# Attention's output projection for two tiles as seven block products instead of eight (Strassen's scheme), with the weights and sums of them streamed in pieces

## The chip, the cores and the metric

The kernel runs on one core of one Trainium2 chip. The metric is device microseconds (us) of one execution, and what is compared is the median of several executions. The engines of the core are named as in the profile: PE is TensorE (matmul), PEld its weight load, DVE is VectorE, ACT is ScalarE, POOL is GpSimd, SP is SyncE. SP and POOL issue the DMA transfers of the part that matters here (SPq is SP's issue queue).

## The reference, cut to what is computed

The model is three layers over `x` of 64 sequences x 32 tokens x 512 features (2048 rows), all in float32. The change lies in the third layer's attention (32 query heads, 8 key heads, 128 per head, a paged cache of 512 keys per sequence), in the last line of this:

```
q = rope(rmsnorm(x @ Wq.T));  k = rope(rmsnorm(x @ Wk.T));  v = x @ Wv.T
probs = softmax(where(valid, q k_all * SCALE, -1e30))
o = einsum('bhqk,bkhd->bqhd', probs, v_all).reshape(bsz, seqlen, HQ * D)
return einsum('bse,de->bsd', o, Wo)
```

`o` is 2048 x 4096 and `Wo` is 512 x 4096: the output projection is a product of 2048 x 4096 by 4096 x 512. A second feed-forward part follows it (the class `Tail` in the kernel).

## The kernel before, in words

**Order of the layers.** `layer0`, `layer1`, then `attention`, whose last act is `tail.run()`, the feed-forward part behind attention. TensorE's instructions have a fixed order: `on_pe` (line 82) ties each one to the one emitted before it. The instructions of the other engines and of the queues are placed by the framework's scheduler when the program is built, by priority in the order of emission and by its estimate of what is ready, so their order can differ a little from the order of the code.

**Steps.** Attention goes over the heads in two halves (`HALVES`, 16 query heads and 4 key heads each) and in each half over 16 tiles of 128 rows (4 sequences): 32 steps (line 858). A step has 16 turns, one for each sequence (4) and key head of the half (4). Turn `i` transposes the softmaxed scores (`turned`, line 805), emits the scores of turn `i + 2` (`scores`, line 779: two matmuls, a DVE reduction, ACT's exponential, a DVE reciprocal and a DVE scaling) and multiplies probabilities by values (`values`, line 820). The tile `sc` in PSUM has one buffer, so a turn's scores can be written once DVE has reduced those before.

**Slots.** Between these pieces each turn has two slots, 32 in a step (line 933): lists of small functions that are emitted there. They hold the projections of the next step (`Projection.product`, six products of two parts each: v, k and four groups of q), the transposes of its queries and keys (`turned`, line 742), loads, and the output projection of the step before (`Output.product`, line 757).

**The output projection.** For one tile and one half it is 16 matmuls (one for each head) of 128 x 128 stationary (`oT`, attention's output, transposed) by 128 x 512 moving (`wo`): eight parts of two heads, accumulated in one PSUM tile `py`, at slots 18, 19, 21, 23, 25, 27, 29, 31 of the following step; the parts of step 30 at the odd slots up to 15 of step 31, and those of step 31 behind the loop (lines 994 to 998). Behind the eighth part DVE copies the result (first half of the heads) or adds what the first half had stored (`y_before`), and SP stores it. `wo` (16 x 512 for each of 128 partitions, one half of the heads) stays in SBUF: it is loaded in four transfers of 1024 KB at the start and in four more between the halves (`output_weights`, line 852). In the profile every float32 matmul of the code is two MATMUL instructions, so a part is four instructions.

**Keys and values.** The keys of a sequence come as 16 transfers of 64 KB by SP, one for each page (`load_keys`, line 649, `kts` has two buffers), emitted at the second turn of the sequence two before; the values come as four indirect transfers by POOL (`load_values`, line 659).

## Time and profile before

| what | value |
|---|---|
| three runs | 3680.55, 3685.11, 3684.99 us; median 3684.99 us |
| the profiled execution's own time | 3681.84 us |
| its span, first to last instruction | 3679.8 us |
| busy: PE, DVE, ACT, POOL | 3631.7, 1805.6, 1316.3, 1254.1 us |
| granted clock of TensorE, mean | 0.999 |
| attention, 1062 to 3509.3 us of the span: PE busy | 2437.35 of 2447.30 us |
| the output projection's matmuls (`py<-wo,oT`, x1024): PE busy | 480.3 us |
| mean share of the 16 DMA engines in attention | 0.44, at 130 GB/s |

How to read it: matmuls are pipelined and the page models their ends, so the records of two neighbours overlap, and the mean duration of one (593 ns for 512 columns) is longer than the distance from its start to the next. Where the prediction needs the cost of a matmul, it takes that distance, from views in order of time. The clock of 0.999 says that PE ran unthrottled throughout. Idle time of an engine that is not the bottleneck costs nothing, so the 480.3 us of the output projection count in full and most of the other engines' times don't.

### The profile page before, as it was taken

The numbers are of one execution on the slowest core, as the hardware profiler recorded it, in microseconds if no ns is written. First come the engines' busy times: TensorE is split into PE (matmuls) and PEld (weight loads), VectorE is DVE, ScalarE is ACT, GpSimd is POOL, SyncE is SP. The second block draws the span as 40 slices with busy tenths as digits, with TensorE's granted clock in tenths as the row PEclk, the third lists the DMA queues.
The fourth block names the chain that finished last, engine by engine and source line by source line (L and its number), as shares of the span: only waits on it lengthen the run. The fifth ranks groups of instructions, "written<-read, shape, count | busy, mean of one in ns | idle before, by whom it ended". The sixth has DMA issues, their size and how long they took to land.

```text
span 3679.8 us, 62184 instructions
## 1 busy us (share of the span) xinstructions
PE 3631.7 (99%) x18752; PEld 2523.7 (69%) x18752; DVE 1805.6 (49%) x4815; ACT 1316.3 (36%) x3014; POOL 1254.1 (34%) x1265
## 2 busy tenths in 40 slices
PE   8999999999999999999999999999999999999999
PEld 3444788888867776777777776777777777777755
DVE  5452222222236655565556655566555655566423
ACT  1111111111125444444444444444444444444411
POOL 0112100000035444544445444444444444454222
PEclk9999999999999999999999999999999999999999
DMA  5014211111144444344443355544444344444521
GB/s 209 23 35 162 92 44 60 44 47 34 37 141 134 124 122 122 117 116 116 123 122 118 115 184 179 165 132 119 123 123 125 117 123 122 129 120 123 160 68 61
DMA packets 410062, 407.70 MB, mean 111 GB/s; under 512 B 49954, under 2 KB 322338, under 8 KB 409730
## 3 DMA queue, kind: packets, MB, share of 16 engines
q1 hardware_dynamic: 363010, 251.65, 22.5%
q0 software_dynamic: 44416, 147.88, 13.2%
q10 hardware_dynamic: 2304, 4.20, 0.3%
q8 instruction: 153, 2.51, 0.3%
q14 instruction: 179, 1.47, 0.1%
HBM read 382.57 MB, written 20.97 MB: 110 GB/s over the span
## 4 chain that ended last, share of the span: by engine, by line
PE 89%; SPq 1%; DMA 0%; DVE 0%; issue 0%; ACT 0%; POOL 0%; ACTq 0%; POOLq 0%; DVEq 0%
PE po L640 14%; PE sc L791 13%; PE pq L640 12%; PE py L640 12%; PE gate_up L311 10%; PE prT_ps L635 6%; PE pz L311 5%; PE po L1100 3%; PE pv L640 3%; PE pk L640 3%; PE po L311 2%; PE qkT_ps L635 2%; PE pd L247 1%; PE ph L122 1%; SPq L93 0%
## 5 line engine op out<-in xcount | busy, mean ns | idle before, releaser
L662 POOL DMA_INDIRECT vt<-in_v_rows,v_rows x512 | 500.7, 978 | 816.7 <-PE po L640 708.8
L640 PEld LDWEIGHTS po<-prT,vt 128*128 128x128 f32 x4096 | 530.1, 192 | 183.7 <-issue 178.0
L796 DVE CUSTOM_DVE_ANT_0 pr<-sc,mask 128x544 f32<-128x544 f32 x512 | 369.2, 721 | 458.7 <-PE sc L791 457.5
L798 ACT ACTIVATE pr<-pr,low 128x544 f32<-128x544 f32 x512 | 383.4, 749 | 540.7 <-DVE low L796 536.4
L791 PE MATMUL sc<-kt,qT 128*128 128x288 f32 (+1 forms) x2048 | 555.1, 394 | 5.2 <-ACT qT L748 2.4
L640 PE MATMUL po<-prT,vt 128*128 128x128 f32 x4096 | 540.8, 275 | 1.6 <-ACT prT L809 1.6
L791 PEld LDWEIGHTS sc<-kt,qT 128*128 128x128 f32 x2048 | 369.2, 191 | 180.8 <-issue 106.9
L640 PE MATMUL py<-wo,oT 128*128 128x512 f32 x1024 | 480.3, 593 | 0.7 <-ACT oT L839 0.7
L640 PE MATMUL pq<-wq,xT 128*128 128x512 f32 x1024 | 480.9, 593 | 0.0
L809 ACT COPY prT<-prT_ps 128x512 f32<-128x512 f32 x512 | 298.5, 583 | 272.6 <-PE prT_ps L635 269.4
L803 DVE TENSOR_SCALAR pr<-pr,low 128x512 f32<-128x512 f32 x512 | 364.5, 712 | 16.7
L635 PE MATMUL prT_ps<-ident,pr 128*128 128x128 f32 x2048 | 310.9, 275 | 1.3 <-DVE pr L803 1.3
L640 PEld LDWEIGHTS py<-wo,oT 128*128 128x128 f32 x1024 | 192.6, 191 | 137.5 <-issue 125.6
L640 PEld LDWEIGHTS pq<-wq,xT 128*128 128x128 f32 x1024 | 182.8, 191 | 129.9 <-issue 125.1
L800 DVE RECIPROCAL low<-low 128x1 f32<-128x1 f32 x512 | 83.5, 163 | 360.6 <-ACT pr L798 359.6
L635 PEld LDWEIGHTS prT_ps<-ident,pr 128*128 128x128 f32 x2048 | 237.7, 141 | 9.1 <-issue 1.5
L126 POOL TENSOR_TENSOR rs<-rs,minus_half 128x4 f32<-128x4 f32 x160 | 166.2, 1039 | 167.4 <-DVE rs L678 166.1
L694 POOL TENSOR_TENSOR rot<-rot,swapped 128x512 f32<-128x512 f32 x160 | 202.7, 1267 | 1.0
L801 ACT ACTIVATE own_pr<-pr,low 128x32 f32<-128x32 f32 x512 | 164.2, 321 | 106.3 <-DVE low L800 104.2
L695 POOL TENSOR_TENSOR rot<-rot,rs 128x512 f32<-128x512 f32 x160 | 177.1, 1107 | 8.0
L395 DVE TENSOR_TENSOR sg<-sg,gate_up 128x256 f32<-128x256 f32 (+1 forms) x88 | 37.1, 421 | 277.3 <-ACT sg L394 277.3
L677 DVE TENSOR_REDUCE rs<-squares 128x4 f32<-128x512 f32 x160 | 109.6, 685 | 118.9 <-ACT squares L675 116.3
(208 smaller groups left out, 4649.8 us busy)
## 6 DMA issues: line engine op xcount, KB each, us to landing
kt<-in_kT SPq DMA_DIRECT2D x2048, 64.0 KB
xt<-x SPq DMA_DIRECT2D x48, 256.0 KB
wq<-in_WqT SPq DMA_DIRECT2D x12, 1024.0 KB
A<-in_A SPq DMA_DIRECT2D x64, 152.0 KB
sets<-in_cond0T SPq DMA_DIRECT2D x32, 256.0 KB
vt<-in_v_rows,v_rows POOLq DMA_INDIRECT x512, 3.7
wo<-in_WoT SPq DMA_DIRECT2D x8, 1024.0 KB
y<-y SPq DMA_DIRECT2D x32, 256.0 KB
```

Source lines behind the costliest of these rows:

```text
L126: self.nc.gpsimd.tensor_tensor(t, t, self.minus_half[:, :n], ALU.pow)
L311: c.on_pe(nc.tensor.matmul(out, lhsT, rhs, start=start, stop=stop))
L635: c.on_pe(nc.tensor.transpose(pt[:, m, :], piece, c.ident))
L640: c.on_pe(nc.tensor.matmul(out, lhsT, rhs, start=first and i == 0, stop=last and i == len(pairs) - 1))
L662: nc.gpsimd.indirect_dma_start(out=vts[b % 2][:, n, :], out_offset=None, in_=a["v_rows"], in_offset=bass.IndirectOffsetOnAxis(ap=rows[h][: ...
L694: nc.gpsimd.tensor_tensor(r, r, tmp, ALU.add)
L695: last = nc.gpsimd.tensor_tensor(r, r, rs.unsqueeze(2).to_broadcast([P, REP, HD]), ALU.mult)
L791: c.on_pe(nc.tensor.matmul(sc[:, lo + n * PSIZE:lo + m * PSIZE].rearrange("p (n k) -> p n k", k=PSIZE), q, kt[:, n:m, g, :], start=True, s ...
L796: nc.vector.tensor_tensor_reduce(pr[:, :NK], sc[:, lo:lo + NK], masks[h, b], -SCALE, 3.0e38, ALU.add, ALU.min, low[:, 0:1])
L798: nc.scalar.activation(pr[:, :NK], pr[:, :NK], AF.Exp, bias=low[:, 0:1], scale=-1.0, accum_out=low[:, 1:2])
L803: nc.vector.tensor_scalar(pr[:, :L], pr[:, :L], low[:, 2:3], None, ALU.mult)
L809: nc.scalar.copy(prT, pt)
```

## The change

Two tiles of one half are projected together. With A the two tiles' rows (two row blocks of 128, two blocks of 8 heads) and B the half's weights (two blocks of 8 heads, two of 256 columns), the eight block products become seven (Winograd's form): A11 B11, A12 B21, S1 T1, S2 T2, S3 T3, S4 B22 and A22 T4, with S1 = A21 + A22, S2 = S1 - A11, S3 = A11 - A21, S4 = A12 - S2, T1 = B12 - B11, T2 = B22 - T1, T3 = B22 - B12, T4 = B21 - T2. A block product is eight matmuls of 128 x 128 by 128 x 256, in two parts of four; a pair of steps has 14 parts.

- The sums of weights T1 to T4 are made once for each half by DVE (`sum_up`, 16 rounds, in steps 0 and 1: two loads of 256 KB, four subtractions of 128 x 256, one store of 512 KB to DRAM).
- `wo` is no longer kept: each part takes a piece of 512 KB (`wo_piece`, rows of 1 KB) from `WoT` or from the stored sums, into one of four buffers; the next piece is asked for in the slot behind each part.
- S1 and S3 are made by POOL at slot 4 of the next even step (behind the loop: by DVE), S2 and S4 by DVE behind the parts that use the sum before.
- Seven products are taken out of PSUM by DVE (five) or ACT (two); POOL makes two additions of 128 x 256 on the results and, in the second half, two of 128 x 512 with what the first half had stored; then both tiles are stored together.
- Where things stand: the parts of a pair lie at slots 18 to 31 of the next even step and 1 to 8 of the odd one; those of the last but one pair at slots 24 to 30 of step 30 and 1 to 19 of step 31, those of the last pair, 14 parts, behind the loop. Steps 0 and 1 have none. In odd steps the projections of the next step stand at slots 10 to 29, with v last.
- A sequence's keys are loaded in four quarters: one where all 16 stood, the others through a list `later`, of which each slot emits at most two entries.

The diff, without its empty lines and with further cuts marked:

```diff
-              "q": wp.tile([P, KC, HQP * HD], F32, name="wq"),
-              "o": op.tile([P, HQP, D], F32, name="wo")}
+              "q": wp.tile([P, KC, HQP * HD], F32, name="wq")}
...
-        def load_keys(h, b):
-            pages = c.numbers(a["pages"][0:1, b * NPP:(b + 1) * NPP], PAGES)
-            for n in range(NPP):
+        def load_keys(h, b, parts=range(4)):
+            if 0 in parts:
+                pages[:] = c.numbers(a["pages"][0:1, b * NPP:(b + 1) * NPP], PAGES)
+            for n in range(parts[0] * NPP // 4, (parts[-1] + 1) * NPP // 4):
                 c.load_by(kts[h, b][:, n, :], a["kT"][ds(pages[n], 1), h].rearrange("a d f -> (a d) f"))
...
+        H = D // 2
+        KH = HQP // 2
+        QH = KH // 2
+        ORDER = (1, 2, 5, 6, 7, 3, 4)
+        ahead = 4
+        def wo_tile():
+            return op.tile([P, QH, H], F32, name="wo", bufs=ahead)
+        def sum_up(h, k):
+            w, t = [], []
+            def rows():
+                w.append(wo_tile())
+                for n in range(2):
+                    at = (h * HQP + n * KH + k) * HD
+                    nc.sync.dma_start(w[0][:, 2 * n:2 * n + 2, :].rearrange("p a b -> p (a b)"),
+                                      a["WoT"][at:at + HD, :])
+            def add():
+                t.append(wo_tile())
+                (b11, b12, b21, b22), (t1, t2, t3, t4) = ([v[0][:, n, :] for n in range(4)] for v in (w, t))
+                nc.vector.tensor_tensor(t1, b12, b11, ALU.subtract)
+                nc.vector.tensor_tensor(t3, b22, b12, ALU.subtract)
+                nc.vector.tensor_tensor(t2, b22, t1, ALU.subtract)
+                nc.vector.tensor_tensor(t4, b21, t2, ALU.subtract)
+            def store():
+                nc.sync.dma_start(sums[h][:, k], t[0])
+            return rows, add, store
+        def wo_piece(h, m, u):
+            w = wo_tile()
+            if m in (1, 2, 3):
+                k, n = {1: (0, 0), 2: (1, 0), 3: (1, 1)}[m]
+                at = (h * HQP + k * KH + u * QH) * HD
+                src = a["WoT"][at:at + QH * HD, n * H:(n + 1) * H].rearrange("(k p) n -> p k n", p=P)
+            else:
+                src = sums[h][:, u * QH:(u + 1) * QH, {5: 0, 6: 1, 7: 2, 4: 3}[m], :]
+            nc.sync.dma_start(w, src)
+            return w
+        class Outputs:
+            def __init__(self, n):
+                self.h, self.n = steps[2 * n][0], n
+                self.T = [steps[2 * n + i][1] for i in range(2)]
+            def first_sums(self, engine):
+                self.o = [oTs.pop(2 * self.n + i) for i in range(2)]
+                (_, _), (o21, o22) = self.blocks = [(o[:, :KH, :], o[:, KH:, :]) for o in self.o]
+                self.s = qp.tile([P, KH, P], F32, name="o_sum", bufs=1)
+                engine.tensor_tensor(self.s, o21, o22, ALU.add)
+                engine.tensor_tensor(o21, self.blocks[0][0], o21, ALU.subtract)
+            def next_sum(self, m, u):
+                (o11, o12), _ = self.blocks
+                q = slice(u * QH, (u + 1) * QH)
+                if m == 6:
+                    nc.vector.tensor_tensor(self.s[:, q], self.s[:, q], o11[:, q], ALU.subtract)
+                else:
+                    nc.vector.tensor_tensor(self.s[:, q], o12[:, q], self.s[:, q], ALU.subtract)
+            def befores(self):
+                self.before = [c.load(wk, "y_before", [P, D], y_part(T), bufs=2) for T in self.T]
+            def product(self, i):
+                m, u = ORDER[i // 2], i % 2
+                if m == 1 and u == 0:
+                    self.y = [wk.tile([P, D], F32, name="y", bufs=2) for _ in range(2)]
                 if u == 0:
-                    self.acc = ps.tile([P, D], F32, tag="mm", bufs=2, name="py")
-                    if self.h:
-                        self.before = c.load(wk, "y_before", [P, D], y_part(self.T))
-                part(self.acc, [(self.oT[:, n, :], self.w["o"][:, n, :]) for n in (2 * u, 2 * u + 1)],
-                     u == 0, u == HQP // 2 - 1)
-                if u < HQP // 2 - 1:
+                    self.acc = ps.tile([P, D], F32, tag="mm", bufs=2, name="py")[:, :H]
+                (o11, o12), (o13, o22) = self.blocks
+                lhs = {1: o11, 2: o12, 3: self.s, 4: o22, 5: self.s, 6: self.s, 7: o13}[m]
+                w = wos.pop(0)
+                part(self.acc, [(lhs[:, u * QH + n, :], w[:, n, :]) for n in range(QH)], u == 0, u == 1)
+                if u == 0:
                     return
-                y = wk.tile([P, D], F32, name="y")
-                if self.h == 0:
-                    nc.vector.tensor_copy(y, self.acc)
+                (y11, y12), (y21, y22) = [(y[:, :H], y[:, H:]) for y in self.y]
+                if m in (1, 5):
+                    nc.scalar.copy(y12 if m == 1 else y22, self.acc)
                 else:
-                    nc.vector.tensor_tensor(y, self.acc, self.before, ALU.add)
-                self.y = y
+                    out, other = {2: (y11, y12), 6: (y12, y12), 7: (y21, y12), 3: (y12, y12),
+                                  4: (y21, y21)}[m]
+                    nc.vector.tensor_tensor(out, self.acc, other, ALU.add)
+                if m == 7:
+                    nc.gpsimd.tensor_tensor(y12, y12, y22, ALU.add)
+                    nc.gpsimd.tensor_tensor(y22, y22, y21, ALU.add)
+                if self.h and m in (3, 4):
+                    n = m - 3
+                    nc.gpsimd.tensor_tensor(self.y[n], self.y[n], self.before[n], ALU.add)
             def store(self):
-                nc.sync.dma_start((y_out if self.h else y_part)(self.T), self.y)
+                for T, y in zip(self.T, self.y):
+                    nc.sync.dma_start((y_out if self.h else y_part)(T), y)
...
-                load_keys(h, b)
+                load_keys(h, b, range(1))
+                later.extend(partial(load_keys, h, b, range(n, n + 1)) for n in range(1, 4))
...
+        wos, wos_to_come = [], [partial(wo_piece, o.h, m, u) for o in outputs for m in ORDER
+                                for u in range(2)]
+        def next_wo():
+            if wos_to_come:
+                wos.append(wos_to_come.pop(0)())
...
+        def slot(fs):
+            now = later[:]
+            del later[:]
+            for f in now[:2]:
+                f()
+            later[:] = now[2:]
+            for f in fs:
+                f()
...
+                if even:
+                    plan = (("v", 2, 3), ("k", 4, 5), (0, 6, 7), (1, 8, 10), (2, 11, 13), (3, 14, 16))
+                    then = zip(("k",) + GROUPS, (10, 12, 15, 17, 20))
+                else:
+                    plan = (("k", 10, 11), (0, 13, 14), (1, 16, 17), (2, 19, 21), (3, 23, 25), ("v", 27, 29))
+                    then = zip(("k",) + GROUPS, (15, 18, 22, 26, 30))
+                p.first = plan[0][0]
...
-            if s:
-                out = Output(*steps[s - 1], oTs.pop(s - 1), ws)
-                ats = (18, 19, 21, 23, 25, 27, 29, 31) if s + 1 < len(steps) else range(1, 16, 2)
-                for u, at in enumerate(ats):
-                    slots[at].append(partial(out.product, u))
-                if steps[s - 1][0] != h:
-                    for u, at in enumerate((20, 24, 28, 31)):
-                        slots[at].append(partial(output_weights, h, u))
-                if s > 1:
-                    slots[2].append(stores.pop(0))
-                stores.append(out.store)
+            if n == 0:
+                for k in range(KH):
+                    for f, at in zip(sum_up(s, k), (0, 3, 6)):
+                        slots[min(4 * k + at, 2 * per - 1)].append(f)
+            else:
+                out = outputs[n - 1]
+                if even:
+                    slots[4].append(partial(out.first_sums, nc.gpsimd))
+                    if out.h:
+                        slots[12].append(out.befores)
+                    if n == 1:
+                        for at in (8, 10, 12, 14):
+                            slots[at].append(next_wo)
+                if last_pair:
+                    ats = (24, 26, 28, 30) + tuple(2 * per + at for at in range(1, 20, 2))
+                else:
+                    ats = (18, 19, 21, 23, 25, 27, 29, 31) + tuple(2 * per + at for at in (1, 2, 4, 5, 7, 8))
+                for i, at in enumerate(ats):
+                    at -= 0 if even else 2 * per
+                    if 0 <= at < 2 * per:
+                        slots[at].append(partial(out.product, i))
+                        slots[at].append(partial(later.append, next_wo))
+                        if i in (5, 7):
+                            for u in range(2):
+                                slots[at].append(partial(out.next_sum, 6 if i == 5 else 3, u))
+                if not even:
+                    slots[22 if last_pair else 13].append(out.store)
...
-        out = Output(*steps[-1], oTs.pop(len(steps) - 1), ws)
-        stores[0]()
-        for u in range(HQP // 2):
-            out.product(u)
+        out = outputs[-1]
+        out.befores()
+        out.first_sums(nc.vector)
+        for i in range(n_out):
+            out.product(i)
+            next_wo()
+            if i in (5, 7):
+                for u in range(2):
+                    out.next_sum(6 if i == 5 else 3, u)
```

## The prediction, made before the changed kernel was run

> **What bounds the kernel now.** I read the page's busy times and slices first, then the table by stage, then who waits for whom, then the order of time around the output projection.
>
> From the page, busy times, PE's and DVE's slices, and the granted clock:
>
> ```profile
> PE 3631.7 (99%) x18752; PEld 2523.7 (69%) x18752; DVE 1805.6 (49%) x4815; ACT 1316.3 (36%) x3014; POOL 1254.1 (34%) x1265
> ...
> PE   8999999999999999999999999999999999999999
> ...
> DVE  5452222222236655565556655566555655566423
> PEclk9999999999999999999999999999999999999999
> ```
>
> PE is full from the second slice on, and at full clock. By stage, attention (1062 to 3509.3) has PE busy for 2437.35 of 2447.30 us: a matmul taken away there is time won, unless something else becomes late; and only 10 us of idle exist that a change could fill. In two steps of the middle (rows of 76 us: span, then PE, PEld, DVE, ACT, POOL busy, clock, DMA share, GB/s) everything else has room:
>
> ```profile
> 1201.00:1277.00 76.00, 76.00 (x401) 53.79 (x399) 44.61 (x118) 35.53 (x82) 34.58 (x36) 1.00 0.43 123
> ```
>
> **1. The matmuls.** The output projection is 32 steps x 8 parts x 4 instructions = 1024 of 512 columns. In the order of time (start, duration, engine, line) a part lies between scores and values so:
>
> ```profile
> 2201.20 1.08 PE L791 MATMUL sc<-kt,qT 128*128 128x288 f32 x4
> 2202.12 1.88 PE L640 MATMUL py<-wo,oT 128*128 128x512 f32 x4
> 2203.83 1.05 PE L640 MATMUL po<-prT,vt 128*128 128x128 f32 x8
> ```
>
> From 2202.12 to 2203.83 is 1.71 us for four; over longer rows of the chain, sixteen of 512 columns take 6.87 us, 0.4294 us each. The nearest row for 256 columns with a 128 x 128 stationary of its own for each matmul, as the changed kernel has it, is layer 1's, in the chain that ended last:
>
> ```profile
> 885.80 4.32 PE gate_up L311 x20
> ...
> 1026.26 17.27 PE pz L311 x80
> ```
>
> 4.32 / 20 = 0.2160, 17.27 / 80 = 0.2159 us: half of 512's, so the narrower product pays no toll in this trace, and the weight loads stay covered. Before: 1024 x 0.4294 = 439.7 us. After: 16 pairs x 14 parts x 8 = 1792 x 0.2159 = 386.9 us. **Gain 52.8 us.** (Busy records, which overlap, would give 480.3 / 8 = 60.) Seven eighths of 439.7 is 384.7, so nearly the whole eighth comes through.
>
> The Trainium skill speaks against it: "TensorE: Matmul & The Clock Gate", section "Back-to-back issue gap", gives for a stream of weight load and matmul pairs about 81 ns at 128 columns and 131 ns at 512, far from proportional. Between them by a line, 256 would cost 0.75 of 512, an estimate from that page, and the projection would be 1792 x 0.75 x 0.4294 = 577 us, 137 us slower. The trace has 0.2159 against 0.4294 in float32, and I go by it.
>
> **2. Work for the other engines in the middle of the stage.** Per pair of steps (152 us) DVE gains five evacuations of 128 x 256 (0.42 us, the row of layer 1's 128 x 256 products) and four sums of 128 x 512 (0.69, the row of `z<-z,xt`), and loses two of 0.69: +3.5 us beside 89 of 152 busy. ACT gains two copies of 128 x 256 (0.37): 0.7. POOL gains two sums of 128 x 1024 (twice the 1.27 of `rot`: 5.1 us), two of 128 x 256 (about 0.65) and in the second half two of 1.27: 6 to 9 us beside 69 of 152. The sums stand one to two slots ahead of their use (2.4 us each in a step of 75.8), S1 and S3 fourteen and more. What POOL's sums can push back is `rot` of the keys (slot 5, used at slot 10) and its four indirect loads (needed a sequence later); DVE's scaling of scores is slower beside POOL (0.49 us alone, 2.19 once beside `rot`, mean 0.71), which the turns carry today. Covered: 0. If the cover went, POOL's 5 us could at worst hold each pair for some us.
>
> One place is thinner than before. In even steps slots 0 and 1 are empty now, and the last turn of an odd step has transposes alone: two turns of some 2.3 and 4.3 us of PE work, while the chain from scores to transposes takes 3.4 us (below) and that turn also carries DVE's and ACT's copies of the last heads. Two turns ahead leaves about a microsecond. At none of 15 such places a stall, or 1 us: 0 to 15; the nearest row is the empty end of step 0, which entered step 1 without a stall. I take **+3**.
>
> **3. Steps 0 and 1.** Here I expect the main loss. The parts of steps 0 and 1 are gone to the end; the end of step 0 (slots 18 to 31) and, new, the first ten slots of step 1 hold nothing. Twelve turns then have PE work of 2.3 to 2.6 us. DVE's own rhythm in the present empty stretch:
>
> ```profile
> 1144.99 0.72 DVE L796 CUSTOM_DVE_ANT_0 pr<-sc,mask 128x544 f32<-128x544 f32 x1 [0.21 <-PE sc L791]
> 1145.64 0.08 DVE L796 DVE_READ_ACCUMULATOR2_ANT low<- 128x1 f32 x1
> 1146.63 0.16 DVE L800 RECIPROCAL low<-low 128x1 f32<-128x1 f32 x1 [0.91 <-ACT pr L798]
> 1146.83 0.49 DVE L803 TENSOR_SCALAR pr<-pr,low 128x512 f32<-128x512 f32 x1
> 1147.24 0.72 DVE L796 CUSTOM_DVE_ANT_0 pr<-sc,mask 128x544 f32<-128x544 f32 x1
> ```
>
> 2.25 us from one reduction to the next, of which only the 0.91 us waiting for the exponential is free: DVE is just level with PE there. Into this fall 6 of the 16 rounds of weight sums, 4 x 0.42 = 1.7 us each, 10 us. All of it in the gaps (two subtractions fit one gap): 0. Behind the scaling every time: DVE is busy 69% of the stretch now, 20.8 of 30 us, and 20.8 + 10.1 + 10.9 of unfilled gaps is 11.8 over.
>
> Loads press too. A round moves 1 MB, six of them 6 MB in 30 us: 210 GB/s on the 132 of that stretch, 342, and the most that any row shows is 318 at 0.89 share:
>
> ```profile
> 0.00:20.00 20.00, 8.29 (x45) 3.86 (x46) 8.16 (x25) 1.28 (x1) 0.72 (x7) 1.00 0.89 318
> ```
>
> And SP issues a sequence's keys in 8.3 us:
>
> ```profile
> 1103.55 8.29 SPq L98 DMA_DIRECT2D kt<-in_kT  x16
> ```
>
> Four empty turns are 10 us; keys 8.3, two rounds 2.6 (six issues of 0.43) and page numbers 0.6 make 11.5. If a round's rows always stood behind all the keys, DVE would sit at them some 8 us for each of three sequences: 25. The quarters and the scheduler's reordering (DVE's own-value copies stand between a reduction and its reciprocal in the trace, so program order is no law) make that the far end. 0 to 25; by the DVE row, the nearest, I take **+9**.
>
> **4. The weights of the parts.** 14 x 512 KB = 7.3 MB per pair, 48 GB/s on 123; in the 22 slots that hold the parts, 140. A packet of 1 KB took 46 ns in this trace (median of 512), a piece 512 x 46 / 16 = 1.5 us of all engines: share 0.43 plus 0.4 there. Pieces are asked for four parts ahead, at least five slots or 12 us; landing is about 4 us (next paragraph). Covered: 0, the rival below is its failure. The 4 MB loads of `wo` at the two starts go, with no PE wait on them today: 0.
>
> **5. The end.** Behind the loop PE did 8 parts, and now does 14; that is in step 1's sum. The first four products need only the first tile, so the wait for the last copy (0.67 us) goes:
>
> ```profile
> 3495.25 14.00 PE L640 MATMUL py<-wo,oT 128*128 128x512 f32 x32 [0.67 <-ACT oT L839]
> ```
>
> But a part lasts 8 x 0.216 = 1.73 us and eats 512 KB: 303 GB/s, under the 318 of the row above by a hair. Four pieces are there; for each of ten more three parts (5.2 us) lie between the asking and the use. Nearest row for landing: the tail's `x`, asked for at 3489.2 to 3490.1 among 1 MB of loads, used by POOL at 3494.12 after waiting: 4 to 4.9 us. Bounds: -0.7 (all in time) and 10 x 0.8 = 8 if each piece takes 2.5 us (about 210 GB/s, the mean of the first slice of the page). I take **+2**. POOL's last addition delays only a store that the tail reads much later.
>
> By the skill's "DMA: Bandwidth & Descriptors", section "Bandwidth", transfers should be 1 MiB or more; from its 0.95 us for 64 KB and 6.15 us for 1 MB, 512 KB is an estimated 3.4 us, and the end would lose some 17 us. This trace's packets speak for less.
>
> **Sum.** 3681.84 (the profiled execution) - 52.8 + 3 + 9 + 2 = 3643.0. That execution lies within the three runs, 3.2 us below their median; I put the median at **3644 us**.
>
> **Rivals.**
>
> *All hidden.* Steps 2 to 5 cost nothing: 3681.84 - 52.8 - 0.7 = 3628. For it: attention waits for other engines only 10 us today. Against it: the DVE row of the empty stretch.
>
> *The start costs its far end.* 25 in place of 9: 3659, and with 10 of the 15 of step 2 up to 3669. For it: SP's 11.5 us against 10. Against it: the list of quarters.
>
> *Late pieces, every pair: slower.* The pieces share SP with keys. If those issue for 8.3 us ahead of a piece and the loaded engines double the landing to 8, a piece comes after 16.7 us where 11.8 are given: 5 us at the tight spot (slot 31 to 37), 16 pairs, 80 us: 3643 + 80 = 3723. It decides from (52.8 - 14) / 16 = 2.4 us of wait for each pair on. For it: DMA share near 0.8 while parts run, 0.65 being today's most in attention. Against it: SP issues keys for 36 of 76 us, and quarters let a piece pass.
>
> *No change in the work.* Would seven products not be fewer columns? 56 x 256 = 14336 for each pair against 32 x 512 = 16384; `ORDER` has seven. Excluded.
>
> **Chances.** Forecast (3634 to 3653) 0.48; all hidden 0.14; far end of the start (3653 to 3677) 0.18; costs that just eat the gain 0.06; late pieces 0.14. This kernel's measurement can tell about 0.2%, 7.4 us. So faster 0.80, same 0.06, slower 0.14. The range is 3626 to 3680: it leaves out the slower case and slivers of two others.
>
> **What would show it.** `py` x1792 at 0.216 us apart, weight loads hidden; PE idle of about 10 us between 1090 and 1190, ended by DVE reductions or scalings; next to none from step 2 to 29; a last burst of parts of 24 to 27 us. Waits of PE for `wo` in the middle, or 256-column matmuls over 0.22 us apart, would make the prediction wrong; likewise DVE held by POOL's sums in every pair.

## The result: 5.8% slower, and the profile after

The median is 3898.09 us (3894.45 to 3899.73, four executions) against 3682.77 us for the kernel before on the same chip: **ratio 1.0583, 95% interval 1.0565 to 1.0602**. Forecast were 3644 us and a gain; the time lies far above the whole range. The profiled execution took 3894.45 us, with a span of 3892.7 us, 212.9 us more than before.

The page's busy line, PE's slices and the granted clock, for the changed kernel:

```profile
PE 3655.6 (94%) x19520; PEld 2701.1 (69%) x19520; DVE 1928.4 (50%) x4993; ACT 1305.3 (34%) x3046; POOL 1382.1 (36%) x1343
...
PE   8999999999978899999999988999999999999899
...
PEclk9999999999999999999999999999999999999999
```

PE is no longer full: 94% of the span against 99%, with a 7 and 8s at the start of attention (slices 12 to 14), in its middle (24, 25) and at its end (38). And it is busy 24 us longer than before, though its parts should have given back 53 us: PE now waits, and it also works more slowly. (A slice is 97 us long, so the row of the clock shows nothing of that; shorter stretches below do.) Who makes it wait (engine, line, waited for: us in total, times, longest):

```profile
PE py L643 <- DMA wo<-wo_sums: 106.5, 23, 7.7
PE qkT_ps L638 <- ACT own_prT L900: 35.1, 30, 3.5
PE sc L876 <- DVE low L881: 17.6, 5, 7.5
```

Then come 9.6 us of scores for copied queries and 8.6 for weights of the second half's keys. Half of all waits are the pieces of the weights that hold sums; before, no wait in attention was longer than 3 us in total. I set the bounds of stages at the first transposition of scores of a step, and give beside each span what it would be if only the matmul step of the prediction had acted (the parts of steps 0 and 1 gone, 0.2159 us for an instruction of 256 columns elsewhere):

| stage | before, us | by the matmul step | after, us | over that | PE idle, before and after | clock after |
|---|---|---|---|---|---|---|
| steps 0 and 1 | 170.6 | 156.9 | 200.1 | 43.2 | 4.8, 35.3 | 0.93 |
| steps 2 and 3 | 151.7 | 148.4 | 173.4 | 25.0 | 0.0, 17.1 | 0.96 |
| steps 4 to 29 | 1974.0 | 1931.1 | 2099.6 | 168.5 | 1.8, 122.0 | 0.98 |
| steps 30, 31 and the parts behind them | 151.8 | 158.7 | 187.6 | 28.9 | 3.3, 23.9 | 0.95 |

So 265.6 us have to be explained: 212.6 of loss (the four stages), and the 53 that did not show. Idle time of PE is 188.4 of them (198.3 less 9.9). The other 77.2 are instructions that took longer from start to start; the parts alone made up 419.4 us where 386.9 were due.

**One late piece.** The order of time on PE at the start of step 19, an odd step (start, duration, engine, line; in brackets the idle time before it and what ended it):

```profile
2650.25 1.89 PE L643 MATMUL py<-wo,oT 128*128 128x256 f32 x8
...
2659.53 3.78 PE L643 MATMUL py<-wo,oT 128*128 128x256 f32 x8 [6.07 <-DMA wo<-wo_sums]
```

The first line is the pair's ninth part (slot 1), the last its tenth (slot 2). Between them PE stood for 6.07 us, and the tenth part then took 3.78 us in place of 1.89. SyncE's queue in the same time (start, time of issuing, number of DMAs):

```profile
2642.90 9.34 SPq L98 DMA_DIRECT2D kt<-in_kT  x16
2652.34 0.38 SPq L801 DMA_DIRECT2D wo<-wo_sums  x1
```

The tenth piece goes out at 2652.34. Its buffer had been free since the sixth part, some 14 us earlier, but SyncE works through its instructions in order, and ahead of the piece stand a sequence's page numbers and its sixteen loads of keys. The view lists only DMAs, so SyncE seems to stand idle from 2634.85 to 2642.90. It does not. It reads the sixteen page numbers from which the addresses of the keys are made (line 93), and only then comes to the wait ahead of the first load of keys (line 98). From the views of these two lines (instruction, count, shortest/median/longest in ns, start of the first and the last):

```profile
L93 SPq FUSED_REGOPS  x16: 147/147/155, 2638.6 to 2642.4; - x16
L93 SPq SEQ_ASSERT  x16: 18/18/18, 2638.8 to 2642.6; - x16
L93 SPq TENSOR_LOAD <-in_pages_ptr x1: 1598/1598/1598, 2634.9 to 2634.9; - x1
L93 SPq TENSOR_LOAD <-in_pages x1: 2008/2008/2008, 2636.6 to 2636.6; - x1
```

```profile
L98 SPq EVENT_SEMAPHORE  x1: 28/28/28, 2642.8 to 2642.8; - x1
```

Two loads of 1.6 and 2.0 us and 16 pairs of short instructions fill nearly 8 us; the wait for the keys' buffer took 0.03 us. Then the keys are issued for 9.34 us, and only then comes the piece, about 1 us before it was needed. Of its 14 us, about 4.3 went with page numbers and 9.6 with keys. In each of the first 14 pairs the tenth piece goes out 12.9 to 15.0 us after its buffer came free: 3.9 to 5.4 with page numbers, 8.4 to 9.3 with issuing keys, and at most 0.4 in which SyncE did nothing. (The wait for the keys' buffer that the expectations of e1 and e7 speak of is this reading.) Who reads this should not take a gap in a list of DMAs for idle time of the queue's engine.

This reading of page numbers did not come with the change. In steps 4 to 29 of the kernel before:

```profile
L93 SPq TENSOR_LOAD <-in_pages_ptr x105: 837/854/5419, 1383.4 to 3357.5; - x105
L93 SPq TENSOR_LOAD <-in_pages x104: 1702/1826/4227, 1384.4 to 3340.4; - x104
```

With its short instructions one reading takes 7.05 us there (median). In each step of 76 us the four readings make 29 us and the keys 35, so SyncE was engaged for 86% of these steps already, and for 92% after the change (gaps under 0.15 us counted as work).

Stretches of 10 us around the wait (PE, PEld, DVE, ACT, POOL busy, granted clock, DMA share, GB/s):

```profile
2640.00:2650.00 10.00, 10.00 (x70) 8.93 (x69) 5.68 (x18) 5.01 (x12) 2.13 (x2) 1.00 0.29 78
2650.00:2660.00 10.00, 3.93 (x23) 3.44 (x23) 2.51 (x7) 1.86 (x5) 1.90 (x2) 0.87 0.97 303
2660.00:2670.00 10.00, 10.00 (x43) 8.43 (x43) 3.18 (x9) 2.04 (x5) 1.45 (x2) 0.79 0.37 112
```

In the first, the DMA engines have time to spare (0.29); in the second, keys and four pieces come at once (0.97, 303 GB/s), so the piece needs up to 6.8 us to land. In the third, PE works all the time at a granted clock of 0.79, a loss of about 2 us: a part of the wait is paid a second time.

**A wait nobody had looked for.** In odd steps the transposition of queries in slots 22 and 30 stands right behind the transposition of the own probabilities, and both use the one buffer that the tag `tq` has in PSUM:

```profile
2709.91 0.27 PE L638 MATMUL own_prT_ps<-ident,own_pr 128*128 128x128 f32 x1
2711.54 0.63 PE L638 MATMUL qkT_ps<-ident,rot 128*128 128x128 f32 x4 [1.36 <-ACT own_prT L900]
```

**Steps 0 and 1.** VectorE's subtractions for the weight sums wait for rows of `WoT`:

```profile
1128.59 1.06 DVE L783 TENSOR_TENSOR wo<-wo 128x256 f32<-128x256 f32 x1 [5.27 <-DMA wo<-in_WoT]
```

VectorE works in order, so the reductions of scores behind these stand too, and PE's scores behind those (one wait of 7.48 us at 1159.27). The rows come behind keys, as the pieces do (whether that is what makes them late, e9 below takes up). SyncE's queue at the start:

```profile
1066.93 24.54 SPq L98 DMA_DIRECT2D kt<-in_kT  x32
1098.28 0.34 SPq L776 DMA_DIRECT2D wo<-in_WoT  x1
```

Between the two, from 1091.5 on, SyncE again reads page numbers.

**The end**, from the chain that ended last: all fourteen parts of the last pair in one burst, 112 instructions in 24.65 us, 0.220 us each, without a wait for a piece:

```profile
3697.48 24.65 PE py L643 x112
```

### The profile page after: what moved, and what is told of

Its sections match the earlier page's. It is cut to its first block, busy times and chain, and to the rows that moved or that the text cites. A ratio compares the mean times of both kernels' runs of the same rounds, so it can differ in the third digit from the quotient of the medians.

```text
span 3892.7 us, 64554 instructions
## 1 busy us (share of the span) xinstructions
PE 3655.6 (94%) x19520; PEld 2701.1 (69%) x19520; DVE 1928.4 (50%) x4993; ACT 1305.3 (34%) x3046; POOL 1382.1 (36%) x1343
## 2 busy tenths in 40 slices
DMA packets 531034, 533.70 MB, mean 137 GB/s; under 512 B 54178, under 2 KB 441250, under 8 KB 530690
## 4 chain that ended last, share of the span: by engine, by line
PE 71%; SPq 7%; DMA 6%; DVE 5%; issue 3%; ACT 1%; POOL 0%; DVEq 0%; ACTq 0%; POOLq 0%
PE po L643 10%; PE gate_up L311 10%; PE sc L876 9%; PE py L643 9%; PE pq L643 8%; PE pz L311 4%; PE prT_ps L638 4%; SPq L98 4%; PE po L1226 3%; DMA wo<-wo_sums 3%; SPq L93 3%; PE pk L643 3%; PE pv L643 2%; PE po L311 2%; DVE own_vt L674 2%
## 5 line engine op out<-in xcount | busy, mean ns | idle before, releaser
L876 PE MATMUL sc<-kt,qT 128*128 128x288 f32 (+1 forms) x2048 | 572.4, 402 | 36.8 <-DVE low L881 17.6
L643 PE MATMUL py<-wo,oT 128*128 128x256 f32 x1024 | 269.3, 411 | 88.1 <-DMA wo<-wo_sums 88.1
L888 DVE TENSOR_SCALAR pr<-pr,low 128x512 f32<-128x512 f32 x512 | 318.8, 623 | 14.2
L643 PEld LDWEIGHTS py<-wo,oT 128*128 128x128 f32 x1024 | 206.6, 206 | 122.4 <-DMA wo<-wo_sums 92.6
L638 PEld LDWEIGHTS prT_ps<-ident,pr 128*128 128x128 f32 x2048 | 237.7, 142 | 15.8 <-issue 7.4
L126 POOL TENSOR_TENSOR rs<-rs,minus_half 128x4 f32<-128x4 f32 x160 | 167.5, 1047 | 212.9 <-DVE rs L683 211.9
L643 PE MATMUL py<-wo,o_sum 128*128 128x256 f32 x768 | 185.7, 386 | 18.4 <-DMA wo<-wo_sums 18.4
L674 DVE COPY own_vt<-v 32x128 f32<-32x128 f32 x512 | 172.5, 337 | 43.5 <-PE po L643 17.0
```

What stands on the lines that cost most here:

```text
L638: c.on_pe(nc.tensor.transpose(pt[:, m, :], piece, c.ident))
L643: c.on_pe(nc.tensor.matmul(out, lhsT, rhs, start=first and i == 0, stop=last and i == len(pairs) - 1))
L674: nc.vector.tensor_copy(own_vts[b % 2][g * S:(g + 1) * S, g % 2, :], v[j * S:(j + 1) * S, g * HD:(g + 1) * HD])
L876: c.on_pe(nc.tensor.matmul(sc[:, lo + n * PSIZE:lo + m * PSIZE].rearrange("p (n k) -> p n k", k=PSIZE), q, kt[:, n:m, g, :], start=True, s ...
L888: nc.vector.tensor_scalar(pr[:, :L], pr[:, :L], low[:, 2:3], None, ALU.mult)
```

## The experiments

Two theories were to be told apart. **The queue**: pieces, rows and keys (with their page numbers) share SyncE, which works in order; take the pieces off it and the waits go. **The traffic**: 126 MB more in the same time (533.70 against 407.70 MB) make landings long, whatever the queue. Beside them stood single suspects: the sums, the shared PSUM buffer, the empty turns.

The experiments ran on three other chips, on which the kernel before took 3705.6 us (the first four), 3699.7 us (the next four) and 3713.0 us (the last four). I compare by ratios to the kernel before on the same chip.

| run | ratio, 95% interval | what it is |
|---|---|---|
| e1_act | 1.0365 (1.0334 to 1.0395) | ScalarE issues the pieces |
| e2_first | 1.0551 (1.0520 to 1.0581) | pieces ahead of keys on SyncE |
| e3_turn | 1.0676 (1.0645 to 1.0707) | transpositions moved to 21 and 29 |
| e4_kept | 1.0274 (1.0244 to 1.0304) | four pieces kept, no streaming |
| after_again | 1.0660 (1.0633 to 1.0686) | the changed kernel, unaltered |
| e5_nosums | 1.0530 (1.0512 to 1.0547) | no weight sums |
| e6_spread | 1.0653 (1.0633 to 1.0673) | weight sums spread over 17 steps |
| e7_pool | 1.0329 (1.0306 to 1.0351) | GpSimd issues the pieces |
| e8_pool_nosums | 1.0098 (1.0072 to 1.0123) | e7, no sums, transpositions at 23 and 29 |
| e9_full | 1.0192 (1.0167 to 1.0217) | e7, sums spread and on GpSimd's queue, 23 and 29 |
| e10_bare | 1.0057 (1.0039 to 1.0076) | four pieces kept, no sums, 23 and 29 |

### Another queue for the pieces: e1_act

```diff
-            nc.sync.dma_start(w, src)
+            nc.scalar.dma_start(w, src)
```

> The pieces of the output weights are issued by ACT in place of SP; same bytes, same four buffers, same parts. Theory (queue): a piece is late because 16 key transfers stand ahead of it on SP (9 us, after a wait for the keys' buffer). Then PE's 106 us of waits for pieces fall under 25, the granted clock returns from 0.979 to 0.99 or more, and the time falls from 3897 to 3740 to 3780. Rival (load): the DMA engines are too full to land a piece in time, whoever issues it: waits stay over 60 us and the time over 3830. Third possibility: ACT itself is held by waiting for the pieces' buffers, and PE waits for ACT's exponentials or copies instead: the py waits go and others of the same size come.

PE's waits for pieces went from 106 us to almost none (0.4), and the ratio is 1.0365; the 3740 to 3780 us of the queue theory would have been 1.016 to 1.026. PE now waits 49.3 us for ScalarE's copies of transposed scores (`po <- ACT prT`). In 13 of these 23 waits, 30.2 us, ScalarE comes to the copy right behind the issue of a piece, which it could not issue earlier since the buffer was still in use by a part, as here:

```profile
2336.80 0.38 ACTq L801 DMA_DIRECT2D wo<-in_WoT  x1
2337.23 0.32 ACT L886 ACTIVATE own_pr<-pr,low 128x32 f32<-128x32 f32 x1 [9.79 <-issue]
```

The other 19.1 us stand mostly at the start of a step, as in runs where ScalarE issues nothing (after_again, below). The lateness is the queue's, and an engine that computes as well pays for issuing.

### Pieces ahead of keys on the same queue: e2_first

```diff
-                        slots[at].append(partial(later.append, next_wo))
+                        slots[at].append(partial(later.insert, 0, next_wo))
```

with one entry of `later` taken for each slot in place of two.

> The next piece goes to the front of the list of late issues, and a slot emits one entry of it in place of two; all on SP, same bytes, same buffers. Queue theory: a piece passes 8 to 12 of the 16 keys (4 to 6 us), so the 6 us wait in every pair shrinks to 0 to 2 us, and the time falls by 50 to 110 us, to 3790 to 3850. Load theory: the landing is what is long, the wait falls by under 2 us per pair, the time by under 40 us. If the build's scheduler sets the issue order whatever the code says, nothing changes.

The waits for pieces fall to 47.4 us (44.1 for sums, 3.3 for rows of `WoT`), and those of scores for keys rise to 35.2 us, 18 times. The lateness moves from one passenger to the other. The ratio is 1.0551, a smaller gain than the 50 to 110 us of the queue theory (1.029 to 1.045).

### The shared PSUM buffer: e3_turn

```diff
-                    then = zip(("k",) + GROUPS, (15, 18, 22, 26, 30))
+                    then = zip(("k",) + GROUPS, (15, 18, 21, 26, 29))
```

> Two transposes of queries in odd steps stand a slot earlier (21 and 29 in place of 22 and 30), so that they don't follow the transpose of the own keys' probabilities, with which they share the one PSUM buffer. Expected: PE's 35 us of waits for ACT's own_prT copies fall under 5 and the time by 30 to 40 us, to about 3862; the waits for pieces stay (over 90 us). Rival: the rotated queries are not ready a slot earlier, PE waits for POOL there instead, and the time stays within 10 us.

The 35 us of `qkT_ps <- ACT own_prT` are gone, and the time is no better (1.049 was expected): 12.0 us of the converse wait came (`own_prT_ps <- ACT qT`: in 21 and 29 the queries stand just ahead of the own probabilities). PE also waits 51.4 us for ScalarE's copies of scores, but that wait need not come of the move: with `po <- issue` it is 68.1 us here and 57.6 in the unaltered kernel on a sister chip (below), and on this chip the unaltered kernel was not run. By itself this settles nothing, since PE was late at the pieces anyway; e8 takes the question up.

### No streaming at all: e4_kept

The first four pieces are loaded once and used for all parts, so the products are not those of the reference.

```diff
-                wos.append(wos_to_come.pop(0)())
+                piece = wos_to_come.pop(0)
+                if len(kept) < ahead:
+                    kept.append(piece())
+                wos.append(kept[(-1 - len(wos_to_come)) % ahead])
```

> Only the first four pieces are loaded and every later part multiplies by one of them again (so most of the output projection uses wrong weights); the parts, the sums, the additions and the stores stay. What is left is the change without its streaming. Expected: no waits of PE for pieces, DMA share in the middle back to about 0.43, a pair of steps 151 us (148.4 of work, 2.2 of own_prT waits, 0.3), clock 0.99 or more, time about 3745: 3897 less 106 of waits, less some 30 of slow clock, less the late weights between the halves (10). Rival: the pairs' extra is not the streaming (engines' additions, clock): over 3800.

1.0274, between the expected 3745 us (1.017) and the rival's 3800 (1.032): of the changed kernel's loss (1.0660 on a sister chip) streaming costs 0.039, but without it the kernel is still slower than before. Taking the pieces off SyncE (e7, below) is worth 0.033 of that 0.039, which leaves about 0.006, give or take 0.005, for the traffic of the pieces as such.

### The changed kernel again: after_again

> The changed kernel unaltered, on the chip of this group, so that the others have it beside them. If the late pieces and keys are the cause everywhere, the ratio to the kernel before is 1.058 within 0.004 and PE waits for the pieces about 106 us. The runs of the first four experiments came from another chip than the first pair, and there a stall of 1.2 to 3.4 us stood at the first turn of each even step, where slots 0 and 1 are empty; if that belongs to the change and not to the experiments, it shows here as well wherever the kernel before is slower than 3690 us, and the ratio is then 1.06 to 1.07.

1.0660, above the first chip's interval, as was expected for a chip on which the kernel before is slower. The waits for pieces are a little smaller (88.4 us), and a wait is there that the first chip did not show: PE stands at the values early in each even step, as in step 10:

```profile
1929.47 1.16 PE L643 MATMUL po<-prT,vt 128*128 128x128 f32 x8 [1.94 <-issue]
```

In all 57.6 us of `po <- ACT prT` and `po <- issue`, nearly all at the start of a step, where the first chip had 1.5.

### No weight sums: e5_nosums

Rows, subtractions and stores of the sums are left out, and the pieces that hold sums are read from the weights, so the products are not those of the reference.

```diff
-                for k in range(KH):
-                    for f, at in zip(sum_up(s, k), (0, 3, 6)):
-                        slots[min(4 * k + at, 2 * per - 1)].append(f)
+                pass
```

> Leaves out the sixteen rounds of weight sums of steps 0 and 1 (rows, subtractions, stores); the four pieces that hold sums are read from the weights instead. Theory: of the 36 us that steps 0 and 1 cost more than they should, the rounds make most: DVE's subtractions waiting for rows that stand behind keys on SP hold up the reductions. Steps 0 and 1 fall from 166.6 to 130-140 us, the ratio by 0.007 to 0.010. Rival: the empty turns of these steps bind by themselves (chain from scores to transposes, SP's 8.3 us of keys): steps 0 and 1 stay above 155 us. The waits for pieces in the middle stay at about 100 us under both.

Steps 0 and 1 fall from 203.4 to 171.9 us, by 31.5 where the theory had 27 to 37 and the rival less than 12, and the ratio falls by 0.013, more than the 0.007 to 0.010 expected. The sums are most of what the start lost; the empty turns alone cost little.

### The sums spread out: e6_spread

Eight rounds in the projections' slots of steps 0 and 1, one in slots 0, 3 and 6 of each even step from 2 to 16. Since the buffers hold a round before, the first four pieces of a pair are asked for at slots 8 to 14 of its even step.

```diff
-                for k in range(KH):
-                    for f, at in zip(sum_up(s, k), (0, 3, 6)):
-                        slots[min(4 * k + at, 2 * per - 1)].append(f)
+                for k in range(KH // 2):
+                    for f, at in zip(sum_up(0, s * KH // 2 + k), (0, 3, 6)):
+                        slots[(10 + 5 * k if s else 4 * k) + at].append(f)
```

> The rounds of weight sums of the first half go to those slots of steps 0 and 1 that hold projections, eight rounds in place of sixteen; the second half's stand one in each even step from 2 to 16, in the buffers that wait there for the next pair. Theory: steps 0 and 1 come within 5 us of the kernel without sums, and the middle loses nothing: the ratio is within 0.002 of that kernel's. Rival: a round in a step's slots 0 to 6 disturbs the parts that stand in slots 1 to 8 only in odd steps, so not at all, but its rows stand ahead of keys on SP and make them late: 2 us for each of eight steps more.

The theory failed. Steps 0 and 1 become only 12.5 us shorter (190.9 us), and steps 4 to 29 become 19.0 us longer (2165.0 against 2146.0), much as the rival had it: 1.0653, no change. But the edit did less than it says. Four of the first eight rounds are written for step 1, and yet the scheduler put all eight into step 0: they end at 1162.1 us, against 1163.5 for the first eight of the unaltered kernel, and step 1 begins at 1180.2. What left steps 0 and 1 are seven later rounds. VectorE still waits 22.1 us for rows there, against 29.3. Whether rounds that are really spread would cost less was not tried.

### GpSimd's queue for the pieces: e7_pool

```diff
-            nc.sync.dma_start(w, src)
+            nc.gpsimd.dma_start(w, src)
```

> GpSimd's queue issues the pieces in place of SyncE's. Theory (piece 9 is late since SP stands at the keys' buffer and then issues sixteen loads of keys ahead of it): PE's waits for pieces fall from 106 us below 25, as they did when ScalarE issued them, without ScalarE's stalls (49 us of PE behind copies), since GpSimd is busy a third of the time: ratio 1.02 to 1.035. Rival one: GpSimd, held at a buffer, is late with the rotation and the indirect loads of values: new waits of 1 to 3 us per pair, ratio 1.035 to 1.05. Rival two: the pieces' transfer time and not the queue binds (they landed in 6.6 us at 303 GB/s): waits stay above 60 us.

1.0329, as the theory said; PE's waits for pieces are 1.8 us. The same place as above, start of step 19, now on PE:

```profile
2616.01 1.89 PE L643 MATMUL py<-wo,oT 128*128 128x256 f32 x8
...
2619.07 1.89 PE L643 MATMUL py<-wo,oT 128*128 128x256 f32 x8
```

and in the order of time of SyncE's and of GpSimd's queue:

```profile
2589.74 23.35 SPq L98 DMA_DIRECT2D kt<-in_kT  x25
```

```profile
2604.49 0.79 POOL L801 DMA_DIRECT2D wo<-wo_sums  x1 [0.66 <-PE py L643]
```

The tenth piece goes out at 2604.49, 14.6 us ahead of its use at 2619.07, while SyncE is still at keys and page numbers, and the tenth part takes 1.89 us again. In steps 4 to 29 the parts fall from 340.5 to 318.1 us from start to start: 22.4 us that had been the slow clock behind waits. In all 121 us, of which 87 are the waits themselves. (New are waits for keys, 25.2 us in place of 3.6, 15 of them in step 15.)

The same bytes moved, but not in the same way: a piece goes as 128 packets of 4 KB from GpSimd's queue and as 512 of 1 KB from the two others. From the pages of e7_pool and e1_act:

```profile
DMA packets 445020, 533.70 MB, mean 139 GB/s; under 512 B 54179, under 2 KB 326563, under 8 KB 444675
```

```profile
DMA packets 531035, 533.70 MB, mean 139 GB/s; under 512 B 54179, under 2 KB 441251, under 8 KB 530691
```

e1 has the changed kernel's packets and its waits for pieces are gone too, so neither bytes nor packets are the main cause of the waits: the second theory, traffic, is out as such.

### Three losses at once: e8_pool_nosums

e7 and e5 together, and the turned queries at 23 and 29. The sums are not computed.

```diff
-                    then = zip(("k",) + GROUPS, (15, 18, 22, 26, 30))
+                    then = zip(("k",) + GROUPS, (15, 18, 23, 26, 29))
```

> GpSimd issues the pieces, the rounds of weight sums are left out as before (the four pieces with sums come from the weights, so that part of the result is not computed), and two transpositions of queries in odd steps move from slots 22 and 30 to 23 and 29, off the own-probability transposition that uses the same PSUM buffer. Theory: the three losses add up, since they stand in different places: 0.033 for the queue (measured), 0.013 for the sums (measured), 0.009 for the buffer (36 us of PE waits, so far unproven): ratio about 1.066 - 0.055 = 1.011, from 1.006 to 1.016. Rival: the buffer's waits only hide others (the experiment that moved these transpositions to 21 and 29 showed as much): ratio 1.017 to 1.024.

1.0098, where 1.011 was expected: the losses add up. Without a gain from the buffer, e7's 0.0331 and e5's 0.0130 would make 1.0199; the rest, 0.010 (give or take 0.005, from the four intervals), is put down to the moved transpositions, once PE is not late anyway. The waits that e7 had at the shared buffer (36.8 us) are gone, and 10.2 us of the converse wait at slot 29 came. From e4 to e10, which differ by the sums and this move, the same subtraction leaves 0.009. The move was not tried by itself on a kernel without late pieces.

### A complete version: e9_full

All of the result, with rows and stores of the sums on GpSimd's queue too, the queries at 23 and 29, and the rounds spread as in e6, with their rows asked for six slots ahead.

```diff
-                    nc.sync.dma_start(w[0][:, 2 * n:2 * n + 2, :].rearrange("p a b -> p (a b)"),
+                    nc.gpsimd.dma_start(w[0][:, 2 * n:2 * n + 2, :].rearrange("p a b -> p (a b)"),
...
-                nc.sync.dma_start(sums[h][:, k], t[0])
+                nc.gpsimd.dma_start(sums[h][:, k], t[0])
```

> Computes all of the result: GpSimd issues the pieces, and the rows and stores of the weight sums too; the sums' rounds stand apart (four in each of steps 0 and 1, in slots that hold projections, one in each even step from 2 to 16) with their rows asked for six slots ahead and not three; transpositions moved as in the kernel without sums. Theory: a round stalls PE only because DVE waits for rows that stand behind up to 32 keys on SyncE's queue; off that queue a round costs its 1.7 us of DVE beside other work, and this kernel is within 0.003 of the one without sums. Rival: the rounds' transfers or GpSimd's time bind: 0.006 to 0.012 above it.

1.0192, 0.0094 above e8: the rival's range, not mine. Steps 0 and 1 still take 190.7 us, against 166.6 without sums. The first stretch of step 0 (columns as above), one of VectorE's subtractions, and VectorE's waits for rows in steps 0 and 1:

```profile
1062.00:1075.00 13.00, 11.41 (x26) 4.96 (x27) 7.85 (x23) 2.17 (x4) 11.14 (x17) 1.00 0.93 286
```

```profile
1079.62 0.42 DVE L782 TENSOR_TENSOR wo<-wo 128x256 f32<-128x256 f32 x1 [5.56 <-DMA wo_sums<-wo]
```

```profile
DVE wo L782 <- DMA wo<-in_WoT: 13.3, 3, 4.9
```

VectorE still waits for rows, and once for a store to free a buffer. The rounds' transfers (with the first 32 keys they fill the DMA engines to 0.93) or GpSimd's own work (busy for 11.14 of 13 us) may hold them; no run separates the two. All eight rounds of steps 0 and 1 are done by 1120, inside step 0 and long before the slots that I wrote them in: the scheduler moves ready work forward, so a slot is no promise, and the spreading was not tested here either. Off SyncE's queue the rounds cost steps 0 and 1 24.1 us (against e8); on it, in e6, 19.0 us (against e5). So for the rows, other than for the pieces, the queue by itself is not shown to be the cause.

### What the matmuls alone are worth: e10_bare

e4 without sums and with 23 and 29; products and sums are not those of the reference.

> Neither streams nor sums weights (four pieces loaded once, used for all products, so the result is not computed), transpositions moved: what is left of the change is its matmuls, the sums of blocks of attention's output and the additions behind the products. By the prediction's own working this should be faster than the kernel before by nearly the 52.8 us of the matmul step: ratio 0.986 to 0.99. By what the runs show so far it is not: 1.0274 with all but the streaming, less 0.013 for sums and 0.009 for the buffer, gives 1.005, and the rest would be the stall of 1.2 to 3.4 us in each even step that these chips show and the first did not (about 50 us, 0.014), and the start's empty turns.

1.0057, by the runs' sum and not by the prediction's. Steps 4 to 29 of it beside those of before_again, which ran on the same chip: the parts take 316.4 us in place of 358.6, **42.2 us less; the prediction's step gives 13 pairs x 3.30 = 42.9**. But PE's idle time rises from 15.0 to 47.3 us, and scores, values and their transpositions take 15.6 us longer from start to start (230 to 234 ns for one of scores, 104.4 to 105.5 for one of values, 111 to 113 for one of the transpositions). The gain is there and is given back. PE's waits in e10_bare, whole run:

```profile
PE po L643 <- issue: 21.0, 19, 2.7
PE po L643 <- ACT prT L894: 14.2, 8, 3.5
```

Most of both stands at the start of the even steps, where slots 0 and 1 are empty. Three others are of 10 us each: reductions, keys, and own probabilities behind the queries of slot 29 (`own_prT_ps <- ACT qT`, 13 times).

### The kernel before on such a chip: before_again

> The kernel before, unaltered, for its profile on this chip, where it has been 15 to 23 us slower than on the first. If the stall of PE for values behind ScalarE's copy belongs to the chip, it stands here too, once in each step or two, about 15 to 25 us in all; if it belongs to the change, PE waits in attention are about 10 us as in the first profile, and the chip's 15 to 23 us lie elsewhere.

```profile
PE po L640 <- ACT prT L809: 13.6, 7, 3.4
```

With 5.1 us of `po <- issue` that is 18.7 us of the stall at the values, against 1.6 in the first profile: the change did not bring it. But the changed kernel has 57.6 of it and e10_bare 35.2; that the emptier turns let more of it through is likely and not shown. What holds ScalarE and VectorE there is open. In after_again both wait for TensorE's signal although the records of the matmuls in question end over a microsecond earlier, and a load of instructions falls into only 3 of the 23 such stalls of over a microsecond.

No version tried beats the kernel before.

## Why the prediction was wrong, step by step

1. **The matmuls: right.** 0.2159 us was forecast for an instruction of 256 columns; undisturbed stretches give 0.216 to 0.220, and e10_bare 42.2 of 42.9 us. The estimate of 0.75 of a 512-column instruction, worked out from the Trainium skill, "TensorE: Matmul & The Clock Gate", section "Back-to-back issue gap", does not hold here: 0.2173 against 0.4310 us (316.4 / 1456 and 358.6 / 832) is 0.504.
2. **Work beside PE: "Covered: 0" held for the additions, the thin place did not.** No wait names the block sums or evacuations for more than some tenths. The thin place was put at +3 (0 to 15) and named rightly, the start of the even steps. The first chip showed next to nothing there (1.5 us), the others 35 us and more. Missed altogether was the wait of 35.1 us at the single `tq` buffer: I costed the moved transpositions as instructions and did not ask which buffer they share and what was written to it just before.
3. **Steps 0 and 1: too small by 34 us.** +9 (0 to 25) was forecast; these steps lost 43.2, and 25.0 went in steps 2 and 3. The far end was worked out as rows that stand behind keys, "8 us for each of three sequences"; the trace has 35.3 us of idle time and a clock of 0.93 on top. I called it far since I trusted the scheduler to reorder and the quarters to let rows pass. Neither did. And the sum of SyncE's work against four empty turns, 11.5 us against 10, has 0.6 for page numbers where the kernel before takes 7.05: by that row it was 18 against 10.
4. **The weights of the parts: the step that failed. "Covered: 0"** rested on a landing of 4 us and an asking of at least 12 us ahead. The landing was 6.8 us in the tight place; the asking was the larger error. I counted from the slot where the request is *written* to its use, and should have counted from where SyncE *gets to it*: in the tight place it read page numbers until 2642.6 and issued keys for 9.34 us, 14 us from the piece's buffer coming free to its issue. The term behind it is the page numbers, 0.6 us in the prediction and 7.05 in the kernel before: "SP issues keys for 36 of 76 us", the argument against the rival, left out the 29 us in which SyncE reads them. "Quarters let a piece pass" was the other argument; the code appends the quarters ahead of the piece, so in that slot nothing passes.
5. **The end: right.** +2 (-0.7 to 8) for pieces at the end; the burst had no wait, at 0.220 us per instruction, 0.5 us over 14 parts. The 28.9 us of that stage lie ahead of the burst, 15.8 of them at pieces and 6.3 at reductions of scores.

The **rival "late pieces, every pair"** was right in mechanism and sign, and I gave it 0.14. It was priced at 5 us for each of 16 pairs, 80 us, at slot 31 to 37; measured were 106.5 us of waits, mostly 5 to 6 us in slot 2 of odd steps, asked for in slot 27. Its price lacked two terms: the page numbers, and the clock. Behind a wait of 6.07 us the granted clock was 0.79 and the next part took twice its time; e7 got 121 us back for 87 us of waits.

What the runs account for, in ratios: the queue 0.033, the sums 0.013 and, as what is left by subtraction, the shared buffer 0.010, from 1.0660 to e8's 1.0098 on another chip; streaming by a free queue is the 0.004 from there to e10's 1.0057. Left in e10 against the 0.986 of the prediction's working are 0.02: PE's idle time and slower neighbours, whose cause on these chips stays open. On the first chip no such kernel ran, so whether the bare change would win there was not tried.

## What to carry to other kernels

When a change streams something, follow each request through its queue: the time ahead of its use begins when the queue's engine reaches it, after all that stands earlier in the queue, and that is more than DMAs: reading addresses into registers took SyncE nearly as long as issuing the loads that use them, and a list of DMAs does not show it. Waits of PE of over 3 us cost more than their length, since the clock falls behind them; and a step that is moved brings its PSUM buffer with it. Where one engine is at 99% and its neighbours look free, a saving on it of 1.4% is gone as soon as a single wait of 3.3 us appears in each pair of steps.

## What the runs showed of the hardware

- A wait of PE of over 3 us in mid-kernel lowers its clock. Waits of 6.07, 4.99 and 3.39 us were followed by parts of 3.78, 3.50 and 3.78 us in place of 1.89; the slow stretch ended within some microseconds (clock 1.00 from 2670 on). The Trainium skill, "TensorE: Matmul & The Clock Gate", section "Why this matters for your kernels", says not to let PE idle for more than about 3 us between bursts, or the clock falls to half; this trace agrees but for one wait: in attention of the changed kernel 25 of the 26 waits of 3.09 us and more were followed by 4 us at a clock of 0.50 to 0.66, one of 3.77 us by a clock of 1.00, and so were all 21 waits of 0.98 to 1.96 us.
- Reading sixteen page numbers into SyncE's registers took 7.05 us in the kernel before and 7.85 in the changed one (medians over attention), beside some 8.3 to 9.3 us for issuing the sixteen loads.
- Which queue issues a DMA mattered more than its transfer. The Trainium skill's "DMA: Bandwidth & Descriptors", section "Issuing engines are not separate DMA queues", holds that several issuing engines save only the time of issuing, usually small; here issuing a piece took about 0.4 us on SyncE (median 0.385 for those of sums) and 0.75 to 0.86 on GpSimd, and yet the dearer queue was faster by 0.033 of the time, since what it saves is the standing behind others.
- Chips differ: the kernel before took 3682.8, 3699.7, 3705.6 and 3713.0 us on four chips, and a stall in it took 1.6 us on the first and 18.7 on the last, in one profile each.
